# Third-level products in all pairs of the first round, index operations split over four steps, conv tiles and unit matrix in ring slots

## The chip, the cores and the metric

The kernel runs on one core of one Trainium2 chip. The metric is the device time of one execution in microseconds (us), as the median of several runs. PE is TensorE, DVE is VectorE, ACT is ScalarE, POOL is GpSimd and SP the engine whose queue issues most transfers. All data are float32.

## The reference

`x` has 32 samples of 128 channels by 2048. Two layers follow each other; cut to what matters:

```python
# layer 0
att  = softmax(mlp(cond))                               # 32 x 8
aggw = einsum('bk,koi->boi', att, weight)               # one 128 x 128 matrix per sample
y    = einsum('boi,bih->boh', aggw, x) + (att @ bias_k)[:, :, None]
x    = x + y @ W.T + bias + sum_e coeffs*scales * (y @ A_e.T) @ Bf_e.T
# layer 1
z = grouped_conv1d(x, 9 taps, 4 groups) + ctx + bias
t = z[:, perm].reshape(rows, 16 heads, 128)
t = down_h(gelu(up_h(t)))                               # 128 -> 512 -> 128 in each head
x = x + unpermuted(t)
```

The low-rank terms are added into the weights, so the dense part of layer 0 is one product of 4096 rows by a 2048 x 2048 matrix. It is taken before the 128 x 128 mixing of each sample.

## The kernel before

**The large product.** Weights and rows are cut in two by two blocks, and the product is made of seven block products instead of eight (the Winograd form of Strassen's scheme). These outer products are the seven *rounds*, in the order `ROUNDS = ("P1", "P2", "P6", "P7", "P5", "P3", "P4")`. A round runs over the eight groups `g` of four samples, so there are 56 *steps* `i`, with `i = 8 * round + g`. Inside a step the same scheme is used again: seven inner products P1 to P7, each of four 128x512 matmuls (`kc` 0 to 3) that are summed in one PSUM bank. In the profile a float32 matmul is two records. The scheme needs combined inputs. `x_combine` makes those of the rows (tile `s_P`, POOL, four operations of 128x512), `inner_weights` those of the weights (tiles `P_t`, POOL).

**The third level.** `PAIRS` names, for each round, the pairs of groups (0 is groups 0 and 1) that go a level further. In such a pair the inner products P2 and P4 of both groups are taken together as seven *quarter* products of four 128x256 matmuls each. `third_weights` prepares their weights once a round: eight POOL operations of 128x256 (tile `P_q`) at once, and four DVE operations of 128x512 put into `quarter_ops`, of which one is issued at each of the places `between(0)` to `between(3)` of the next step. `third_inputs` prepares the rows of a pair (tile `sq`, four operations of 128x512). A step of such a pair runs `multiply_third` in place of `multiply`: five products P1, P5, P6, P3, P7, and in the odd group the seven quarters too. In the rounds of `ENDS` (P1 and P4) the quarters stand after the five products, in the others between them. A quarter's result is added by one DVE operation. The result tiles of both groups are stored after the odd step. `multiply` takes seven products in the order P1, P2, P6, P5, P7, P3, P4.

A product that continues in a bank (P6 continues in the bank of P1, P3 in that of P5, and so on) can start only when the DVE or ACT operation that reads the bank's sum so far is done. This is how a late DVE operation holds up PE.

**What else stands in the steps.** The order of the instructions is the program's own order, written out by hand; each engine runs its queue in that order. Steps 0 to 5 begin with `w_make_two`, which makes two further blocks of the weights: 14 matmuls of 128x512 with a DVE addition after each (line 226), then a store to DRAM from POOL's queue. The callback `between(j)` puts further DVE work after the products. In the first round that is a `row_sums` of a weight block at j = 1 and j = 3 (line 243, two operations of 128x1024), and at j = 5 of the first four steps two additions to `wsum` (lines 1140 and 1141). At j = 2 it issues from SP the loads of the weight blocks of a later step. After each step the generator `small()` is advanced, twice a step from step 5 on: it holds small work (attention, bias, conv weights), and last of all the index operations on `row` and `orow` (lines 997 to 1005), 13 DVE operations of 128x16 in one piece.

**Memory.** Nearly all large tiles come from one pool of `SLOTS` buffers of 8 KB per partition (`slot`). A load into a reused buffer waits for the last reader of what was there. The unit matrix `ident` and the three conv tiles `cq`, `cs`, `cr` have memory of their own.

**The rest.** The last round overlaps the mixing (line 601) and the conv (line 693) with its steps; after it 128 heads of the second layer run `ffn_up` (line 837) and `ffn_down` (line 848), with gather and scatter by indirect transfers whose rows are in `row` and `orow`.

Of the kernel before, what the change touches and what calls it, by code (L numbers as in the profile page):

```python
# [8 lines left out]
FP = mybir.dt.float32  # L9
# [7 lines left out]
P = 128  # L17
B = 32
L = 2048
QW = 512  # L20
# [4 lines left out]
NPH = 4  # L25
# [6 lines left out]
GB = 4  # L32
NG = B // GB
GT = GB * P
SLOTS = 25

# [10 lines left out]


PAIRS = {
    "P1": (2, 3), "P2": (0, 1, 2), "P6": (0, 1, 2, 3), "P7": (0, 1, 2, 3),
    "P5": (0, 1, 2, 3), "P3": (0, 1, 2, 3), "P4": (0,),
}
ENDS = ("P1", "P4")
# [3 lines left out]
def adaln_ffn_kernel(  # L59
# [16 lines left out]
    nc = tc.nc  # L76

    dram = ctx.enter_context(tc.tile_pool(name="dram", bufs=1, space=DRAM))
    const = ctx.enter_context(tc.tile_pool(name="const", bufs=1))
    agp = ctx.enter_context(tc.tile_pool(name="agp", bufs=2))  # L80
    big = ctx.enter_context(tc.tile_pool(name="big", bufs=SLOTS))
    psum = ctx.enter_context(tc.tile_pool(name="psum", bufs=1, space=PSUM))
    banks = [psum.tile([P, QW], FP, name=f"bank{i}", tag=f"bank{i}") for i in range(8)]

    def slot(name, shape=(P, L)):
        return big.tile(list(shape), FP, name=name, tag="s")


    def bank():
        return banks.pop(0)  # L90

    def done(*ps):
        banks.extend(ps)
# [22 lines left out]
        for g in range(NG)  # L116
    }

    ident = const.tile([B, B], FP, name="ident", tag="ident")
    make_identity(nc, ident)  # L120
    mix = const.tile([P, KEXP, P], FP, name="mix", tag="mix")
    att_bc = const.tile([P, B * KEXP], FP, name="att_bc", tag="att_bc")
    aggb = const.tile([P, B], FP, name="aggb", tag="aggb")
# [6 lines left out]
    cs = const.tile([P, 4], FP, name="cs", tag="cs")  # L130
# [422 lines left out]
    late, ins, pms, xgs, x1ts, va, vb, hts, open_ = {}, {}, {}, {}, {}, {}, {}, {}, {}  # L553
# [135 lines left out]
    def conv_product(ps, k, i, v, first, last):  # L689

        for r, (out, rhs) in enumerate(zip(halves(ps), halves(v))):
            w = late["tw"][:, k - 1] if 1 <= k <= 4 else late["te"][:, k // 5]
            nc.tensor.matmul(  # L693
                out, lhsT=w[:, 2 * i + r], rhs=rhs,
                start=first and r == 0, stop=last and r == 1, skip_group_check=True,
            )

    def biased(out, ps, c, i, bias, scale):

        for r in range(2):  # L700
            for j in range(2):
                part = slice((2 * r + j) * NM, (2 * r + j + 1) * NM)
                b = 2 * c + j
                nc.scalar.activation(
                    out[:, part], ps[:, part], AF.Identity,
                    bias=bias[:, 2 * i + r, b : b + 1], scale=scale,
                )

    def conv_tile(c, i, name):
        return agp.tile([P, QW], FP, name=f"{name}_{c}{i}", tag=name, bufs=1)  # L710

    def conv_begin(c, i):
        px, py = bank(), bank()
        v = va[c, i]
        conv_product(px, 1, i, v[:, 0], True, False)
        conv_product(py, 3, i, v[:, 2], True, False)
        q, s = conv_tile(c, i, "cq"), conv_tile(c, i, "cs")
        biased(q, px, c, i, ctxb, 2.0)
        nc.scalar.mul(s, py, 2.0)
        open_[c, i] = px, py, q, s  # L720

    def conv_middle(c, i):
        px, py, q, s = open_[c, i]
        v = va[c, i]
        conv_product(px, 2, i, v[:, 1], False, False)
        conv_product(py, 4, i, v[:, 3], False, True)
        r = conv_tile(c, i, "cr")
        biased(r, py, c, i, ctxb, 2.0)
        nc.vector.tensor_tensor(q, q, px, ALU.subtract)
        nc.vector.tensor_tensor(s, s, py, ALU.subtract)  # L730

        nc.vector.tensor_tensor(v[:, 2], px, r, ALU.add)
        done(py)
        open_[c, i] = px, q, s, r
# [39 lines left out]
    def stage_second(c, n):  # L774
        if n in (6, 9):
            conv_middle(c, int(n == 9))
        if n in (5, 8):
            conv_inputs(c, int(n == 8), 1)
        if n in (0, 2):
            mix_begin(2 * c + n // 2)  # L780
# [5 lines left out]
    def third_products(c, n):  # L786
        if n in (5, 8):
            conv_begin(c, int(n == 8))
        if n in (6, 9):
            conv_end(c, int(n == 9))  # L790
        if n in (0, 2):
            mix_work(2 * c + n // 2)
# [71 lines left out]
        ws.append(t)  # L864

    def late_loads():
        late["tw"] = slot("tw_l", (P, 4, GR, P))
        nc.sync.dma_start(late["tw"].rearrange("p k r c -> p (k r c)"), tw_d)
        late["w1"] = slot("w1", (P, NPH, QW))
        nc.sync.dma_start(late["w1"].rearrange("p f n -> p (f n)"), w1_d.to_broadcast([P, L]))  # L870
        late["fb"] = slot("fb", (P, NPH, QW))
        nc.sync.dma_start(
            late["fb"].rearrange("p f n -> p (f n)"), fbias.to_broadcast([P, L])
        )


    def small():
# [3 lines left out]
        def take(rows, cols):  # L881
            used[0] += cols
            return sm[0:rows, used[0] - cols : used[0]]
# [8 lines left out]
        adiag = take(B, B * KEXP)  # L892
        ones = take(P, P)
        nc.gpsimd.memset(ones, 1.0)
        yield

        p0 = bank()
# [55 lines left out]
        for o in range(NPH):  # L953
# [44 lines left out]
        nc.vector.tensor_scalar(  # L998
            orow[:, 0], pos, 0x1FC, None, ALU.bitwise_and
        )  # L1000
        nc.vector.tensor_scalar(orow[:, 1], pos, 9, None, ALU.logical_shift_right)
        nc.vector.tensor_tensor(row, row, orow[:, 0], ALU.add)
        nc.vector.tensor_tensor(row, row, orow[:, 1], ALU.add)
        for g in range(NG):
            nc.vector.tensor_scalar(orow[:, g], pos, g * L, None, ALU.add)
        yield


    ctx.enter_context(tc.manual_schedule())
# [44 lines left out]
    unsummed, unsummed_first = [], list(first)  # L1054
    olds = {}
    chain = small()
    nxt, waiting, ts, quarter_ops = {}, {}, {}, []
    heads = [(g, h) for g in range(NG) for h in range(NH)]
# [5 lines left out]
    for i, (r, g) in enumerate(steps):  # L1064
# [45 lines left out]
        if last_round and g == 0:  # L1110
            quarters, quarter_ops = third_weights(r, rhs)
            late_loads()
# [148 lines left out]
```

## Time and profile before

| | us |
|---|---|
| median of 3 runs | 2588.83 (2587.49 to 2589.33) |
| profiled execution | 2590.78 |
| its span | 2589.0 |
| PE busy in the span | 2574.6 (99%) |
| DVE busy | 1514.5 (58%) |
| POOL busy | 1362.8 (53%) |
| ACT busy | 532.2 (21%) |
| first round, from its first product to its end | 45.50 to 297.83 |
| second round begins | 297.83 |

A row of a timeline gives the start in the span, the time until the group's last instruction ends, engine, line, operation, output and inputs by name, shape and count, and in brackets how long the engine stood idle before it and what ended that. Consecutive equal instructions are merged in one row. Starts that follow each other show the pace; the duration of one instruction overlaps the next one by a little.

### The profile page before, as it was taken

The numbers are of one execution on the slowest core, as the hardware profiler recorded it, in microseconds if no ns is written. First come the engines' busy times: TensorE is split into PE (matmuls) and PEld (weight loads), VectorE is DVE, ScalarE is ACT, GpSimd is POOL, SyncE is SP. The second block draws the span as 40 slices with busy tenths as digits, with TensorE's granted clock in tenths as the row PEclk, the third lists the DMA queues.
The fourth block names the chain that finished last, engine by engine and source line by source line (L and its number), as shares of the span: only waits on it lengthen the run. The fifth ranks groups of instructions, "written<-read, shape, count | busy, mean of one in ns | idle before, by whom it ended". The sixth has DMA issues, their size and how long they took to land. (4 is left out here: it accounts for less than half of the span.)

```text
span 2589.0 us, 21703 instructions
## 1 busy us (share of the span) xinstructions
PE 2574.6 (99%) x6998; PEld 1328.4 (51%) x6998; DVE 1514.5 (58%) x2368; ACT 532.2 (21%) x1099; POOL 1362.8 (53%) x1124
## 2 busy tenths in 40 slices
PE   9999999999999999999999999999999999999999
PEld 4445554455555555555554454455544454455543
DVE  5656565466555676654377666667666666666601
ACT  0000000000000000000011244444444444444432
POOL 7323756988977845977514234343444334434222
PEclk9999999999999999999999999999999999999999
DMA  7543467778467477573766887777767877787432
GB/s 324 210 163 129 162 235 317 289 296 336 187 246 296 189 316 297 199 317 156 254 229 228 256 303 254 241 243 232 228 225 234 258 232 222 226 257 234 161 127 89
DMA packets 186577, 608.30 MB, mean 235 GB/s; under 512 B 17632, under 2 KB 91872, under 8 KB 142304
## 3 DMA queue, kind: packets, MB, share of 16 engines
q1 hardware_dynamic: 147936, 473.48, 50.8%
q0 software_dynamic: 32704, 130.04, 15.0%
q10 hardware_dynamic: 5824, 3.40, 0.4%
q8 instruction: 56, 0.92, 0.1%
q14 instruction: 57, 0.47, 0.1%
HBM read 372.45 MB, written 200.84 MB: 221 GB/s over the span
## 5 line engine op out<-in xcount | busy, mean ns | idle before, releaser
L837 PE MATMUL bank<-t,ws 128*128 128x512 f32 x1024 | 460.3, 592 | 0.0
L848 PE MATMUL bank<-gl,ws 128*128 128x512 f32 x1024 | 460.2, 592 | 0.0
L855 POOL DMA_INDIRECT out<-t,orow x128 | 152.1, 1188 | 538.8 <-DVE t L853 478.6
L840 ACT ACTIVATE gl<-bank 128x512 f32<-128x512 f32 x512 | 305.8, 598 | 418.0 <-PE bank L837 415.4
L447 PE MATMUL bank<-P_t,s_P 128*128 128x512 f32 x704 | 314.5, 595 | 3.0 <-DVE p L440 3.0
L848 PEld LDWEIGHTS bank<-gl,ws 128*128 128x128 f32 x1024 | 194.6, 190 | 233.0 <-issue 231.5
L837 PEld LDWEIGHTS bank<-t,ws 128*128 128x128 f32 x1024 | 194.6, 190 | 226.6 <-issue 222.7
L586 POOL TENSOR_TENSOR x<-x,fb 128x512 f32<-128x512 f32 x128 | 177.1, 1412 | 227.5 <-DMA x<-in_x 159.5
L853 DVE TENSOR_TENSOR t<-bank,t 128x512 f32<-128x512 f32 x128 | 88.4, 690 | 325.0 <-PE bank L848 325.0
L440 DVE TENSOR_TENSOR u<-bank,u 128x512 f32<-128x512 f32 x204 | 134.0, 687 | 233.1 <-PE bank L447 214.1
L592 ACT ACTIVATE bank<-w,aggb 128x512 f32<-128x512 f32 x128 | 80.8, 684 | 867.3 <-DMA w<-w_d 855.0
L447 PE MATMUL bank<-wo_P,s_P 128*128 128x512 f32 x544 | 241.6, 592 | 0.0
L283 POOL TENSOR_TENSOR xt<-xt,xt 128x512 f32<-128x512 f32 x128 | 163.1, 1307 | 107.4 <-DMA xt<-in_xT 89.4
L447 PEld LDWEIGHTS bank<-P_t,s_P 128*128 128x128 f32 x704 | 134.3, 191 | 156.6 <-issue 152.7
L311 POOL TENSOR_TENSOR s_P<-xt 128x512 f32<-128x512 f32 x56 | 73.9, 1319 | 212.4 <-DMA xt<-in_xT 170.5
L565 DVE SCALAR_TENSOR_TENSOR ags<-mix,att_bc,ags 128x128 f32<-128x128 f32 x224 | 181.3, 810 | 4.7
L447 PEld LDWEIGHTS bank<-wo_P,s_P 128*128 128x128 f32 x544 | 103.4, 190 | 116.5 <-issue 113.6
L821 POOL DMA_INDIRECT t<-hx_d,row x128 | 131.2, 1025 | 57.0 <-issue 23.2
L440 DVE TENSOR_TENSOR p<-bank,p 128x512 f32<-128x512 f32 x84 | 56.6, 688 | 116.3 <-PE bank L447 111.6
L693 PE MATMUL bank<-va,tw_l 128*128 128x256 f32 x512 | 122.0, 380 | 2.2 <-DVE va L677 2.2
L447 PE MATMUL bank<-wo_P,xt 128*128 128x512 f32 x272 | 122.3, 592 | 0.0
L460 PE MATMUL bank<-P_q,sq 128*128 128x256 f32 x528 | 120.7, 379 | 0.4 <-DVE u L468 0.4
(191 smaller groups left out, 3515.8 us busy)
## 6 DMA issues: line engine op xcount, KB each, us to landing
xt<-in_xT SPq DMA_DIRECT2D x88, 1024.0 KB, 10.6
u<-u_d SPq DMA_DIRECT2D x40, 1024.0 KB, 10.2
wo_P<-wb_d SPq DMA_DIRECT2D x36, 1024.0 KB, 13.0
u<-c_d SPq DMA_DIRECT2D x64, 512.0 KB, 7.3
x<-in_x SPq DMA_DIRECT2D x32, 1024.0 KB, 9.3
xg<-x SPq DMA_DIRECT2D x256, 128.0 KB, 5.4
hx_d<-x1t SPq DMA_DIRECT2D x32, 1024.0 KB, 6.7
hx_d<-ht SPq DMA_DIRECT2D x32, 1024.0 KB, 4.8
```

The source lines that it names most:

```text
L283: nc.gpsimd.tensor_tensor(out[:, i, j], a[:, i, j], b[:, i, j], op)
L440: nc.vector.tensor_tensor(to, ps, to, ALU.add)
L447: nc.tensor.matmul(ps, lhsT=lhs[k][:, bass.ts(kc, P)], rhs=rhs[k][kc], start=first and kc == 0, stop=last and kc == 3, skip_group_check=True,)
L460: nc.tensor.matmul(out, lhsT=sq[k][:, i, bass.ts(kc, P)], rhs=quarters[i][k][kc], start=first and i == 0 and kc == 0, stop=last and i == 1 ...
L565: nc.vector.scalar_tensor_tensor(ag, mix[:, k], att, ag, ALU.mult, ALU.add)
L586: nc.gpsimd.tensor_tensor(xt[:, f], xt[:, f], late["fb"][:, f], ALU.add)
L693: nc.tensor.matmul(out, lhsT=w[:, 2 * i + r], rhs=rhs, start=first and r == 0, stop=last and r == 1, skip_group_check=True,)
L821: nc.gpsimd.indirect_dma_start(out=t.rearrange("p k t -> p (k t)"), out_offset=None, in_=hx_d[g].rearrange("l k t -> l (k t)"), in_offset= ...
L837: nc.tensor.matmul(pu, lhsT=w[:, m * P : (m + 1) * P], rhs=t[:, 0], start=True, stop=True)
L840: nc.scalar.activation(gl[m], pu, AF.Gelu)
L848: nc.tensor.matmul(pd, lhsT=w[:, (MC + m) * P : (MC + m + 1) * P], rhs=gl[m], start=(m == 0), stop=(m == MC - 1),)
L855: nc.gpsimd.indirect_dma_start(out=out, out_offset=bass.IndirectOffsetOnAxis(ap=orow[:, g, h : h + 1], axis=0), in_=t[:, 1], in_offset=None,)
```

## The change

- The first round takes the third level in all four pairs, not in pairs 2 and 3 alone. Steps 0 to 3 become `multiply_third`, and `third_weights` of this round runs at step 0 in place of step 4.
- The index operations are cut by further `yield`s into six pieces. As the generator is advanced twice after a step, they stand after four steps: 2, 5, 4 and 2 operations after steps 11, 12, 13 and 14.
- The three conv tiles become slices of one ring slot, taken in the last round; the unit matrix becomes a part of the tile `small` and is made on POOL after step 0 in place of the start. The ring has 26 slots in place of 25.

```diff
-SLOTS = 25
+SLOTS = 26
 PAIRS = {
-    "P1": (2, 3), "P2": (0, 1, 2), "P6": (0, 1, 2, 3), "P7": (0, 1, 2, 3),
+    "P1": (0, 1, 2, 3), "P2": (0, 1, 2), "P6": (0, 1, 2, 3), "P7": (0, 1, 2, 3),
     "P5": (0, 1, 2, 3), "P3": (0, 1, 2, 3), "P4": (0,),
 }
-    ident = const.tile([B, B], FP, name="ident", tag="ident")
-    make_identity(nc, ident)
...
-    def conv_tile(c, i, name):
-        return agp.tile([P, QW], FP, name=f"{name}_{c}{i}", tag=name, bufs=1)
+    def conv_tile(n):
+        return late["cv"][:, n]
...
-        q, s = conv_tile(c, i, "cq"), conv_tile(c, i, "cs")
+        q, s = conv_tile(0), conv_tile(1)
...
-        r = conv_tile(c, i, "cr")
+        r = conv_tile(2)
...
     def late_loads():
+        late["cv"] = slot("cv", (P, NPH, QW))
         late["tw"] = slot("tw_l", (P, 4, GR, P))
...
         nc.gpsimd.memset(ones, 1.0)
+        ident = take(B, B)
+        make_identity(nc, ident)
         yield
...
         nc.vector.tensor_scalar(
             orow[:, 0], pos, 0x1FC, None, ALU.bitwise_and
         )
+        yield
         nc.vector.tensor_scalar(orow[:, 1], pos, 9, None, ALU.logical_shift_right)
         nc.vector.tensor_tensor(row, row, orow[:, 0], ALU.add)
+        yield
         nc.vector.tensor_tensor(row, row, orow[:, 1], ALU.add)
         for g in range(NG):
             nc.vector.tensor_scalar(orow[:, g], pos, g * L, None, ALU.add)
-        yield
+            if g % 2 == 1:
+                yield
```

## The prediction

> **What bounds the kernel.** I read the page's engine sums first, then the waits of PE, then the timelines of PE, DVE and POOL around each place that the change touches, and the windows with the granted clock.
>
> ```profile
> PE 2574.6 (99%) x6998; PEld 1328.4 (51%) x6998; DVE 1514.5 (58%) x2368; ACT 532.2 (21%) x1099; POOL 1362.8 (53%) x1124
> PE bank L447 <- DVE p L440: 3.0, 1, 3.0
> PE bank L693 <- DVE va L677: 2.2, 4, 0.9
> ```
>
> PE is busy throughout, so the time moves only by PE work, PE pauses and PE's clock. The second and third lines (us in total, times, longest) are the two largest pauses inside the run; the one of 3.0 us is in the reach of the change. DVE around it:
>
> ```profile
> 390.88 1.29 DVE L440 TENSOR_TENSOR p<-bank,p 128x512 f32<-128x512 f32 x2 [1.83 <-PE bank L447]
> 392.08 1.22 DVE L997 TENSOR_SCALAR row<-pos 128x16 int32<-128x16 int32 x1
> 393.21 1.30 DVE L998 TENSOR_SCALAR orow<-pos 128x16 int32<-128x16 int32 x1
> ...
> 398.10 1.83 DVE L1005 TENSOR_SCALAR orow<-pos 128x16 int32<-128x16 int32 x8
> 399.85 0.68 DVE L440 TENSOR_TENSOR p<-bank,p 128x512 f32<-128x512 f32 x1
> ```
>
> and PE, with the window that shows its clock (the eighth value from the right block, after POOL, is PEclk):
>
> ```profile
> 390.68 3.60 PE L447 MATMUL bank<-w,xt 128*128 128x512 f32 x8
> 394.11 3.60 PE L447 MATMUL bank<-P_t,s_P 128*128 128x512 f32 x8
> 400.67 5.37 PE L447 MATMUL bank<-P_t,s_P 128*128 128x512 f32 x8 [2.97 <-DVE p L440]
> 405.88 7.03 PE L447 MATMUL bank<-w,s_P 128*128 128x512 f32 x16
> 400.00:405.00 5.00, 4.33 (x6) 1.84 (x7) 2.29 (x6) 0.00 (x0) 1.42 (x2) 0.66 1.02 362
> ```
>
> The index operations hold DVE from 392.08 to 399.85. P1's addition, which could run from about 394.4, comes after them; P6 continues in P1's bank, is due at 397.54 and starts at 400.67. After the pause PE is granted 0.66 of its clock, and this product takes 405.88 - 400.67 = 5.21 us where the one before it took 3.43.
>
> **Index operations.** Both losses go: 2.97 + (5.21 - 3.43) = 4.75 us. Each new place has its own deadline. Two operations after step 11 end at 394.43, when P1 itself has just ended: nothing. Five after step 12 cost by the same rows 394.43 to 398.10 and one blocked start more, 5.0 us; with the last additions of the step before (1.4 us) and P1's own (0.7) that is 7.1, and in step 13 P6 is due only after P1, P5 and four quarters, 2 x 3.43 + 4 x 1.73 = 13.8 us. If that step had no quarters between, P6 would be due at 6.87 and PE would lose 0.2. Four after step 13 face step 14, where P6 is due at 6.87: by L1005's eight in 1.83 us they cost 1.0 to 1.3, at 1.3 each 5.2, so 0 to 0.4 us late; I take 0, as L1005 is the same operation. The last two: 0.
>
> **PE work.** A step's seven products go from 81.55 to 105.58, 24.03 us, 3.433 each. The quarters of a pair:
>
> ```profile
> 238.44 1.03 PE L460 MATMUL bank<-w,xt 128*128 128x256 f32 x4
> 241.89 5.34 PE L460 MATMUL bank<-P_q,sq 128*128 128x256 f32 x24
> 250.52 0.97 PE L939 MATMUL bank<-small 128*128 128x32 f32 x8
> ```
>
> from 238.44 to 250.52, 12.08 us for 28 matmuls. A pair falls from 14 products (48.06) to 10 and the quarters (34.33 + 12.08 = 46.41): 1.65 us less, in two more pairs 3.30 us. This is the whole arithmetic gain.
>
> **What is added beside PE.** POOL gets eight `sq` operations of about 1.27 us and the eight `P_q` operations four steps earlier. It stood idle 20.47, 19.96 and 30.54 us before the `x_combine` of steps 2, 3 and 4, and those results are due at the second product of a later step; hidden with over 20 us to spare. DVE gets seven quarter additions of 0.69 for three product additions less per pair; a quarter lasts 1.73, so each is done before the next. The stores of `m_P` wait on SP's queue for the end of the pair, and the x load of step 3 behind them; it is issued near 108 and due near 148, against 10.6 us to land (median of `xt`). The unit matrix leaves a POOL queue that then waits 8 us for DVE anyway. The ring has one slot more until the last round and then 25 again; the order on each engine around the conv is unchanged: 0, with the four waits of L693 (2.2 us) as the bound either way.
>
> **The new wait.** It stands between steps 0 and 1. With five products step 0 ends at 45.50 + 5 x 3.433 = 62.66. PE goes on with `w_make_two`; four matmuls go to free banks, to 66.10, and the fifth continues in the first one's bank, so it waits for that one's addition on DVE. Ahead of it in DVE's queue now stand P3's addition, the fourth `P_q` operation, two row sums, P7's addition and lines 1140 and 1141. `multiply` ran the row sums and those two lines before its last products; five products leave no such room. What the items take depends on POOL:
>
> ```profile
> 191.46 0.73 POOL L393 TENSOR_TENSOR P_q<-w 128x256 f32<-128x256 f32 x1
> 196.08 1.70 POOL L399 TENSOR_TENSOR P_q<-w,w 128x256 f32<-128x256 f32 x1
> 192.77 1.09 DVE L1130 TENSOR_TENSOR P_q<-P_t,P_q 128x512 f32<-128x512 f32 x1
> 193.79 3.41 DVE L243 TENSOR_TENSOR wsum<-wsum,w 128x1024 f32<-128x1024 f32 x2
> 206.11 2.48 DVE L243 TENSOR_TENSOR wsum<-wsum,w 128x1024 f32<-128x1024 f32 x2
> 53.24 7.42 DVE L243 TENSOR_TENSOR wsum<-wsum,w 128x1024 f32<-128x1024 f32 x4
> ```
>
> Beside POOL's small `P_q` operations two row sums take 3.33 (193.79 to 197.12) and a POOL operation of 0.73 takes 1.70; with POOL quiet they take 2.39 (206.11 to 208.50); beside POOL's 128x512 operations the first three of the last row take 6.2, 2.07 each. P3's addition starts 0.27 after its product, 59.50, and the next operation 0.61 later, 60.11. Beside `P_q`: 1.05 + 3.33 + 0.61 + 1.05 + 1.66, and 0.69 for the awaited addition: 68.50, PE goes on 0.14 later, a pause of 2.54 us. Quiet: 0.60 + 2.39 + 0.61 + 0.78 + 1.23 + 0.69: 66.41, pause 0.45. Beside 128x512: 1.21 + 4.14 + 0.61 + 1.21 + 2.07 + 0.69: 70.04, pause 4.08. I take 2.54: POOL ended `x_combine` of step 1 at 58.3, its eight `P_q` operations follow and took 8.8 us from 191.46, so they lie just beside this stretch. Between steps 2 and 3 the same queue without `P_q`, with POOL quiet, ends within 0.1 us of need.
>
> **Does the clock fall again?** By the rows, pauses up to 0.9 us left it alone and one of 2.97 cost 1.78 more; 2.54 lies between, unseen. I take none, and keep 1.78 for the range. The Trainium skill, TensorE: Matmul & The Clock Gate, section "What's actually happening", puts the fall after an idle window of about 3.4 us that runs free of the kernel. This trace fell at 2.97, below that figure; by the page neither pause would cost clock, which by itself would make the sum -3.73 instead of -5.51.
>
> **Sum.** -4.75 - 3.30 + 2.54 = -5.51 us. The profiled execution, 2590.78 (span 2589.0 and 1.78 around it), becomes 2585.3; the median of the runs is 1.95 lower, so 2583.3. 0.2% is 5.2 us, about what a measurement of this kernel can tell from no change: the forecast stands just outside.
>
> **Rivals.**
> - *Free DVE.* POOL gets through earlier, the pause is 0.45: -7.60, 2581.2. For it: DVE idles before 59.5, and POOL can catch up there. Against: POOL has 8.8 us of `P_q` left at 58.3.
> - *Long pause or the clock.* 2.54 with the clock loss gives -3.73, 2585.1; 4.08 with it gives -2.19, 2586.6. For it: `P_q` on DVE and POOL already contend from 46.4 on, which makes `x_combine` end later and puts 128x512 operations beside the row sums.
> - *The index wait only moves.* The five-operation piece stops PE as the thirteen did: -3.30 + 2.54 = -0.76, 2588.1. Against: the 13.8 us above.
> - *Slower: a weight block comes late.* The second block of step 2 now reuses a buffer that is free only after the row sums behind P3 of step 1. They end at 62.66 + 2.54 + 12.02 (`w_make_two`, 69.53 to 81.55) + 4 x 3.43 + 0.27 + 0.61 + 2.39 = 94.2. Step 2 begins 12.02 + 17.17 + 12.08 after 65.20, at 106.47, and needs this block added before its sixth matmul, so landed by 110.2: 16.0 us. Loads of `in_WT` land in 11.0 (median); the slowest first load, of `a_sb`, took 24.9. Such a one would stop PE for 8.9 and cost 1.78 of clock: +5.2, 2594.0. It decides from 16 us on, and turns the sign near 21.
>
> **Numbers.** Forecast 0.45, free 0.28, long or clock 0.17, moved 0.04, slower 0.06. The forecast's own spread is about 1.5 us, two thirds of it beyond 5.2. Faster: 0.30 + 0.28 = 0.58; slower 0.06; the rest, 0.36, within. The range runs from 2580.7 (the free case with some of the L693 waits gone) to 2587.2 (the long pause with clock, and 0.6 for the waits priced at nothing); outside are the moved and the slower case and the tails.
>
> **What would show it.** Right: no index wait near 395, clock 1.00 there, steps 1 and 3 ending in 12.1 us of quarters, a PE pause at L223 near 66 released by DVE's addition to `w`, with L1141 ending just before. Wrong: no pause there (free), a pause over 3 us with a window of lower clock (long), PE waiting for a transfer near 110 (slower), or a pause near 415 or 440 behind `orow` (moved).

## The result and the profile after

The changed kernel takes 2594.2 us (median of 14 runs, 2590.76 to 2596.7) against 2588.3 (14 runs, 2586.43 to 2589.58): 1.0021 times as long, 95% interval 1.0014 to 1.0028. It is slower, where 2583.3 was forecast. The profiled execution is 2594.36 us, its span 2592.6; that of before was 2590.78, some 2.5 above the median of its 14 runs, so the two traces differ by 3.6 us and the medians by 5.9.

The engines' sums on the page after:

```profile
PE 2573.9 (99%) x7046; PEld 1339.0 (52%) x7046; DVE 1525.8 (59%) x2378; ACT 533.0 (21%) x1099; POOL 1376.2 (53%) x1132
```

PE did a little less work, and the time still grew. The waits of PE (us in total, times, longest) say where:

```profile
PE bank L221 <- DVE w L224: 4.9, 3, 2.8
PE bank L458 <- DVE u L466: 3.3, 1, 3.3
PE bank L691 <- DVE va L675: 1.3, 3, 0.6
```

Most line numbers are two lower than before. The index wait on `p` is gone. The first two rows were short before:

```profile
PE bank L223 <- DVE w L226: 0.5, 2, 0.3
PE bank L460 <- DVE u L468: 0.4, 1, 0.4
```

Now the first has 4.9 us in three places and the second 3.3 in one. PE's timeline at four places:

```profile
394.30 3.60 PE L445 MATMUL bank<-w,xt 128*128 128x512 f32 x8
397.73 4.46 PE L445 MATMUL bank<-P_t,s_P 128*128 128x512 f32 x10
...
63.00 3.60 PE L221 MATMUL bank<-bf_sb,a_sb 128*128 128x512 f32 x8
68.37 5.42 PE L221 MATMUL bank<-tb,sa 128*128 128x512 f32 x12 [1.78 <-DVE w L224]
...
208.01 3.70 PE L221 MATMUL bank<-bf_sb,a_sb 128*128 128x512 f32 x8
214.50 5.83 PE L221 MATMUL bank<-tb,sa 128*128 128x512 f32 x9 [2.80 <-DVE w L224]
...
884.19 3.60 PE L445 MATMUL bank<-P_t,s_P 128*128 128x512 f32 x8
891.12 5.18 PE L458 MATMUL bank<-P_q,sq 128*128 128x256 f32 x16 [3.33 <-DVE u L466]
```

The first two rows follow each other at PE's pace: no pause at the index operations. The third and fourth hold the pause that the forecast expected near 66. The last four hold two pauses that it did not name, one in `w_make_two` of step 5 and one in the fifth round, P5, which the diff does not touch. The windows (after POOL stands PEclk) add what those two cost in clock:

```profile
400.00:405.00 5.00, 5.00 (x13) 2.16 (x12) 2.58 (x5) 0.00 (x0) 2.75 (x3) 1.00 1.00 357
215.00:220.00 5.00, 5.00 (x9) 2.11 (x8) 3.38 (x7) 0.00 (x0) 0.00 (x0) 0.67 0.00 0
890.00:895.00 5.00, 3.88 (x11) 3.25 (x12) 4.96 (x9) 0.00 (x0) 4.84 (x5) 0.66 0.01 2
```

In each of the last two windows a third of 5 us is lost, 1.7 us. So the two new places cost 2.8 + 1.7 and 3.3 + 1.7 = 9.5 us, less the 0.3 and 0.4 us at most that PE waited there before. Set against the forecast's -5.51 that gives about +3.3, and the traces show +3.6.

**Why DVE is late at 214.** The changed kernel's DVE and POOL around it, then the same operations of the kernel before (lines 932 and 311 there are 933 and 309 here):

```profile
208.89 4.96 DVE L933 SCALAR_TENSOR_TENSOR aggb<-att_bc,small,aggb 128x32 f32<-128x32 f32 x7
213.77 3.20 DVE L224 TENSOR_TENSOR w<-bank,w 128x512 f32<-128x512 f32 x5
...
207.54 1.26 POOL L309 TENSOR_TENSOR s_P<-xt 128x512 f32<-128x512 f32 x1 [7.00 <-PE bank L445]
211.33 1.26 POOL L312 TENSOR_TENSOR s_P<-xt,s_P 128x512 f32<-128x512 f32 x1
```

```profile
209.83 2.09 DVE L932 SCALAR_TENSOR_TENSOR aggb<-att_bc,small,aggb 128x32 f32<-128x32 f32 x7
211.85 4.30 DVE L226 TENSOR_TENSOR w<-bank,w 128x512 f32<-128x512 f32 x7
...
219.80 1.27 POOL L311 TENSOR_TENSOR s_P<-xt 128x512 f32<-128x512 f32 x1 [13.47 <-PE bank L223]
```

Seven tiny operations on `aggb` take 4.96 us in place of 2.09, while POOL runs `x_combine` of step 6. One by one, the first three take 1.30, 1.19 and 1.18 us, each ending within 0.1 us of the end of a POOL operation, and the other four 0.27, after the last of POOL's. The third and the fourth of the changed kernel:

```profile
211.45 1.18 DVE L933 SCALAR_TENSOR_TENSOR aggb<-att_bc,small,aggb 128x32 f32<-128x32 f32 x1
212.67 0.27 DVE L933 SCALAR_TENSOR_TENSOR aggb<-att_bc,small,aggb 128x32 f32<-128x32 f32 x1
```

In the kernel before POOL did `x_combine` 12 us later: it stood idle 13.47 us until a product of `w_make_two` had released a buffer. With 26 buffers it still waits there, but for an earlier product and 7.00 us.

**Why DVE is late at 890.** After, and before:

```profile
882.63 1.75 DVE L419 TENSOR_TENSOR sq<-xt,xt 128x512 f32<-128x512 f32 x1
884.31 1.75 DVE L420 TENSOR_TENSOR sq<-xt,sq 128x512 f32<-128x512 f32 x1
887.18 1.31 DVE L561 TENSOR_SCALAR ags<-mix,att_bc 128x128 f32<-128x128 f32 x1
889.70 2.47 DVE L466 TENSOR_TENSOR u<-bank,u 128x512 f32<-128x512 f32 x4
...
882.24 1.60 POOL L309 TENSOR_TENSOR s_P<-xt 128x512 f32<-128x512 f32 x1
```

```profile
883.12 1.21 DVE L421 TENSOR_TENSOR sq<-xt,xt 128x512 f32<-128x512 f32 x1
886.58 0.27 DVE L563 TENSOR_SCALAR ags<-mix,att_bc 128x128 f32<-128x128 f32 x1
888.05 2.47 DVE L468 TENSOR_TENSOR u<-bank,u 128x512 f32<-128x512 f32 x4
...
849.69 1.27 POOL L254 TENSOR_TENSOR P_t<-wo_P,P_t 128x512 f32<-128x512 f32 x1 [5.62 <-PE bank L447]
882.61 1.17 POOL L399 TENSOR_TENSOR P_q<-wo_P,wo_P 128x256 f32<-128x256 f32 x1
```

Before, POOL waited 2.23 and 5.62 us for buffers of `P_t` in `inner_weights`, and so was at its small `P_q` operations when DVE did `sq`. After, it is nine microseconds further, at 128x512 operations, and `sq` and `ags` take longer beside them.

### The profile page after: what moved, and what is told of

It is laid out like the page before. It is cut to its first block, busy times and chain, and to the rows that moved or that the text cites. A ratio compares the mean times of both kernels' runs of the same rounds, so it can differ in the third digit from the quotient of the medians.

```text
span 2592.6 us, 21824 instructions
## 1 busy us (share of the span) xinstructions
PE 2573.9 (99%) x7046; PEld 1339.0 (52%) x7046; DVE 1525.8 (59%) x2378; ACT 533.0 (21%) x1099; POOL 1376.2 (53%) x1132
## 5 line engine op out<-in xcount | busy, mean ns | idle before, releaser
L445 PE MATMUL bank<-P_t,s_P 128*128 128x512 f32 x768 | 340.7, 592 | 0.0
L445 PEld LDWEIGHTS bank<-P_t,s_P 128*128 128x128 f32 x768 | 145.9, 190 | 167.5 <-issue 163.8
L563 DVE SCALAR_TENSOR_TENSOR ags<-mix,att_bc,ags 128x128 f32<-128x128 f32 x224 | 187.5, 837 | 4.7
L458 PE MATMUL bank<-P_q,sq 128*128 128x256 f32 x576 | 132.9, 382 | 3.3 <-DVE u L466 3.3
L458 PEld LDWEIGHTS bank<-P_q,sq 128*128 128x128 f32 x576 | 110.4, 192 | 35.1 <-issue 21.1
L691 PE MATMUL bank<-va,tw_l 128*128 128x256 f32 x512 | 122.0, 380 | 1.5 <-DVE va L675 1.3
```

Of the source, the lines that this page charges most:

```text
L445: nc.tensor.matmul(ps, lhsT=lhs[k][:, bass.ts(kc, P)], rhs=rhs[k][kc], start=first and kc == 0, stop=last and kc == 3, skip_group_check=True,)
L458: nc.tensor.matmul(out, lhsT=sq[k][:, i, bass.ts(kc, P)], rhs=quarters[i][k][kc], start=first and i == 0 and kc == 0, stop=last and i == 1 ...
L563: nc.vector.scalar_tensor_tensor(ag, mix[:, k], att, ag, ALU.mult, ALU.add)
L691: nc.tensor.matmul(out, lhsT=w[:, 2 * i + r], rhs=rhs, start=first and r == 0, stop=last and r == 1, skip_group_check=True,)
```

## The experiments

**Theory A:** the 26th buffer frees POOL from waits for buffers; its operations run earlier, and land beside DVE operations that they hold up. **Theory B:** the two new pairs move POOL or overload DVE, and the number of buffers is innocent.

### One part of the change at a time

`e_index` is the kernel before with the further `yield`s alone.

> The kernel before with the index operations in six places and nothing else. Both theories: the pause of 2.97 us before the product at 400.67 and the half clock after it go, 4.75 us in all, so about 2583.5 us, ratio 0.9982. If the wait only moves to one of the new places: 2587 to 2588.

Measured: 2585.03 us against 2588.64, ratio 0.9985 (0.9976 to 0.9994), 3.6 us less. At 394 us PE runs through at clock 1.00. The wait is gone and has not moved.

`e_slots` is the kernel before with the memory part of the diff alone:

```diff
-SLOTS = 25
+SLOTS = 26
...
+        late["cv"] = slot("cv", (P, NPH, QW))
...
+        ident = take(B, B)
+        make_identity(nc, ident)
```

> The kernel before with 26 buffers, the conv tiles and the unit matrix in them; pairs and index operations as before. Theory A (one buffer more lets POOL run ahead, beside short DVE chains, which then hold up PE near 211 and near 887): POOL's x_combine of step 6 starts some 10 us earlier, the aggb operations of line 933 take 1.2 us each in place of 0.27, and there is a new PE pause of about 3 us near 211 or near 887, or both: 2591 to 2597 us, beside the index pause that stays. Theory B (the two new pairs move POOL, not the number of buffers): no change, 2588.3 within 1.5, and no pause there.

Measured: 2597.07 us against 2588.64, ratio 1.0033 (1.0021 to 1.0044), at the top of what theory A gave, with the pairs as before. Its DVE, POOL and waits of PE:

```profile
209.91 4.92 DVE L933 SCALAR_TENSOR_TENSOR aggb<-att_bc,small,aggb 128x32 f32<-128x32 f32 x7
...
208.40 1.38 POOL L309 TENSOR_TENSOR s_P<-xt 128x512 f32<-128x512 f32 x1 [1.75 <-PE bank L445]
```

```profile
PE bank L458 <- DVE u L466: 3.3, 1, 3.3
PE bank L221 <- DVE w L224: 3.2, 2, 2.9
PE bank L445 <- DVE p L438: 2.9, 1, 2.9
```

Both new pauses stand beside the old index pause. The memory part alone makes them; theory B falls.

`t_pairs25` is the kernel before with the new `PAIRS` line alone.

> The kernel before with the third level in all pairs of the first round and nothing else, still 25 buffers. Theory A: the pause near 66 of 1.9 to 2.5 us stands, those near 211 and 887 do not: -3.30 + 2 = -1.3, about 2587 us. Theory B: the pauses near 211 (3.0, and 1.7 of clock) and near 887 (2.9, and 1.7 of clock) come with the pairs: -1.3 + 9.3 = +8, about 2596 us.

Measured: 2603.03 us, ratio 1.0051 (1.0038 to 1.0065), outside what either theory gave. The two pauses are indeed absent, as A says, but a third, larger one stands in step 1 (its PE, its ACT):

```profile
97.80 2.90 PE L447 MATMUL bank<-P_t,s_P 128*128 128x512 f32 x3 [13.02 <-ACT m_P L442]
...
97.07 1.07 ACT L442 COPY m_P<-bank 128x512 f32<-128x512 f32 x2 [30.31 <-DMA wb_d<-w]
```

The result tile `m_P` of step 1 finds no buffer until a store of a weight block has landed, since a pair holds both its result tiles. With 26 buffers nobody waits there. So the extra buffer is what the two pairs need, and what brings the two pauses.

`t_after25` is the changed kernel with `SLOTS = 25`, all else kept.

> The changed kernel with 25 buffers in place of 26. Theory A: the pauses near 211 and 887 go, up to 9.3 us, so 2585 us, and with them the whole of the unforeseen loss. Theory B: both stay, 2594 us.

Measured: 2601.32 us, ratio 1.0047 (1.0033 to 1.006). The two pauses are gone, the wait for `m_P` is there with 12.9 us. In this kernel the waits of POOL are back:

```profile
236.98 1.27 POOL L309 TENSOR_TENSOR s_P<-xt 128x512 f32<-128x512 f32 x1 [17.75 <-PE bank L221]
861.96 1.27 POOL L252 TENSOR_TENSOR P_t<-wo_P,P_t 128x512 f32<-128x512 f32 x1 [5.62 <-PE bank L445]
```

It has the unit matrix and the conv tiles where the changed kernel has them, so those moves alone do not make the pauses; together with `e_slots` this leaves the count of buffers. The wait of 12.9 us also shifts all that follows it; no run has the moves with 25 buffers and without that wait. The 2585 us expected of it was wrong for the same reason as above.

### Is it POOL beside DVE?

`n_comb6` takes POOL away at the first place and leaves DVE its work:

```diff
+        if (r, g) == ("P1", 6):
+            for n, t in enumerate((a21, a11, a22, a12)):
+                nc.scalar.copy(s[:, n], t)
+        else:
+            tt(s[:, 0], a21, a22, ALU.add)
...
```

> The changed kernel with the four operations of x_combine for step 6 as copies on ACT in place of additions on POOL (the additions themselves are left out). DVE has the same work at the same place; only POOL is quiet from 207 to 213. Theory A (a POOL operation with SBUF inputs holds up DVE operations with two SBUF inputs): the aggb chain takes 2.3 us in place of 5.2 and the pause near 211 goes, with its clock: 2589.5 to 2591, as f_aggb. If the chain is slow by itself, or by its place: 5.2 us, pause and 2594 stay.

Measured: 2590.89 us against 2588.63, ratio 1.0004 (0.9995 to 1.0013), 3.6 us better than the changed kernel by the ratios to before. Its DVE (lines below the edit are four higher):

```profile
209.05 2.11 DVE L937 SCALAR_TENSOR_TENSOR aggb<-att_bc,small,aggb 128x32 f32<-128x32 f32 x7
211.07 4.31 DVE L224 TENSOR_TENSOR w<-bank,w 128x512 f32<-128x512 f32 x7
```

The same seven operations at the same place take 2.11 us, and the awaited addition is in time.

`n_p5` does the like at the second place: for step 34 the `pieces` are skipped and `x_combine` is four ACT copies.

> The changed kernel with the x pieces and x_combine of step 34 (POOL from 876.8 to 888.4) as four copies on ACT; the additions are left out. DVE keeps all its work there, the four sq operations of steps 32 and 33 too. Theory A: the sq operations take about 0.7 us each in place of 1.64 to 1.75, ags 0.27 in place of 1.31, the quarter addition at 889.7 is in time, and the pause of 3.3 us and its 1.7 of clock go: 2589 to 2591. If DVE's sq operations are too much at this place whatever POOL does, the pause stays above 2 us: 2592 to 2594.

Measured: 2589.02 us against 2588.41, ratio 1.0000 (0.9991 to 1.0009), 5.3 us better. Its DVE (five lines higher):

```profile
881.36 0.68 DVE L424 TENSOR_TENSOR sq<-xt,xt 128x512 f32<-128x512 f32 x1
881.96 0.68 DVE L425 TENSOR_TENSOR sq<-xt,sq 128x512 f32<-128x512 f32 x1
883.76 0.28 DVE L566 TENSOR_SCALAR ags<-mix,att_bc 128x128 f32<-128x128 f32 x1
884.34 2.48 DVE L471 TENSOR_TENSOR u<-bank,u 128x512 f32<-128x512 f32 x4
```

`sq` falls from 1.75 to 0.68, `ags` from 1.31 to 0.28, and the pause is gone. At both places it is POOL beside DVE, shown and not only argued.

### Keeping the work and removing the pauses

`f_aggb` takes the eight `aggb` operations to the end of the next piece of `small()`:

```diff
-        nc.vector.tensor_scalar(aggb, ab[:, :, 0], bk[:, 0:1], None, ALU.mult)
...
         nc.vector.tensor_scalar(ctx34, ctxb, 0.75, None, ALU.mult)
+        nc.vector.tensor_scalar(aggb, ab[:, :, 0], bk[:, 0:1], None, ALU.mult)
...
```

> The changed kernel with the eight aggb operations two pieces of small() later, where DVE has time before anyone waits for it. Theory A (POOL's x_combine of step 6 beside the aggb chain holds up DVE, and so the product at 214): the pause near 211 goes, 3.0 us and up to 1.7 of clock, so about 2589.5 to 2591. If the addition is late for another reason (DVE has too much work in step 4 whatever POOL does), the pause stays and the time with it, 2594.

Measured: 2589.17 us against 2587.87, ratio 1.0005 (0.9996 to 1.0014): the pause near 211 is gone, 4.6 us less than the changed kernel by the differences to before.

`f_p5` gives POOL the `sq` operations of round P5's first pair:

```diff
-            sq = third_inputs(i, nc.gpsimd if r in ENDS else nc.vector)
+            sq = third_inputs(i, nc.gpsimd if r in ENDS or r == "P5" else nc.vector)
```

> The changed kernel with the four sq operations of round P5's pair 0 on POOL in place of DVE (steps 32 and 33). Theory A (POOL, 8 to 10 us early, stretches the DVE operations ahead of the quarter addition at 890): the pause near 887 of 3.3 us and its 1.7 of clock go, so 2589 to 2591. If POOL is then late itself with sq, PE waits for sq and nothing is gained: 2594 or more.

Measured: 2588.0 us, ratio 1.0000 (0.9991 to 1.0009): 5.8 less, the pause near 887 gone, no wait for `sq`.

`f_sums` issues the first steps' sums earlier:

```diff
-            if ri == 0 and j in (1, 3) and unsummed:
+            if ri == 0 and j in (1, 2 if g < 4 else 3) and unsummed:
...
-            if ri == 0 and j == 5 and unsummed_first:
+            if ri == 0 and j == 2 and unsummed_first:
```

> The changed kernel with the row sums and the additions to wsum of the first four steps one product earlier (at j = 1 and 2 in place of 1, 3 and 5), so that they do not stand behind the last product of a step that has five. The pause near 66 goes, 1.9 to 2.5 us: 2592 to 2592.5. If it is the P_q operations beside POOL that make the awaited addition late, most of it stays: 2594.

Measured: 2591.59 us, ratio 1.0015 (1.0006 to 1.0024): 2.2 less, the pause near 66 gone. The interval overlaps that of the changed kernel, so the trace shows this and not the time alone. POOL's `P_q` operations still run there, so the place of the sums in DVE's queue decides, and the expectation's other reading falls.

`f_all` has all three.

> The changed kernel with the three edits of f_aggb, f_p5 and f_sums. If the three pauses are independent and are the whole of the loss against the forecast: 2594.2 - 3.0 - 1.7 - 3.3 - 1.7 - 2 = about 2582.5 us, under both kernels (before 2588.5). If removing one moves POOL or DVE so that another place stalls: 2586 to 2590.

Measured: 2581.86 us against 2587.87, ratio 0.9974 (0.9965 to 0.9984), and 11.9 below the changed kernel where the three alone sum to 12.6. It beats both kernels. Its longest waits of PE, and its windows at the three places:

```profile
PE bank L155 <- DVE warm L152: 1.5, 1, 1.5
PE bank L691 <- DVE va L675: 1.4, 2, 0.7
PE bank L178 <- DMA bf_sb<-in_BfT: 1.4, 1, 1.4
```

```profile
65.00:70.00 5.00, 5.00 (x13) 2.13 (x12) 4.86 (x9) 0.59 (x1) 4.92 (x7) 1.00 0.01 2
210.00:215.00 5.00, 5.00 (x13) 2.19 (x12) 4.00 (x7) 0.00 (x0) 0.55 (x1) 1.00 0.00 0
885.00:890.00 5.00, 5.00 (x18) 3.15 (x17) 3.59 (x6) 0.00 (x0) 5.00 (x5) 1.00 0.00 0
```

PE is busy for all of each, at full clock.

`f_all_p23` is `f_all` with `"P1": (2, 3)`.

> The kernel f_all with the third level in pairs 2 and 3 of the first round alone, as before the change. It shows what the two new pairs are worth where nothing else is late: by the matmul count 2 x 1.65 = 3.3 us more, so 2585.2 against 2581.9 of f_all. If the pairs bring waits of their own even then, less: 2582 to 2584.

Measured: 2584.12 us against 2588.63, ratio 0.9982 (0.9973 to 0.9991). Between the medians lie 2.3 us, between the differences to before 1.5, and the intervals overlap. The traces show where the gain lies: from the first matmul of `w_make_two` of step 0 to that of step 4 are 145.00 us (33.03 to 178.03) here and 141.61 (34.33 to 175.94) in `f_all`, 3.39 less, as the matmul count says. The two whole spans differ by 1.1 us only (2582.4 and 2581.3): the trace of `f_all` began step 0 1.30 us later, and PE waited 1.9 us at L691 against 0.7. Whether the two pairs bring this about is not shown.

## Why the prediction was wrong

- **Index operations: right.** -4.75 was forecast. Between `e_slots` and the changed kernel the lead at the same matmuls grows from 0.98 to 5.53 us across this place, 4.55; `e_index` shows 3.6, interval 1.6 to 6.2.
- **PE work: right.** -3.30 was forecast, and the stretch with the pairs became 3.39 us shorter, of which the whole time shows 1.5 to 2.3. Step 2 began at 106.45, forecast 106.47; so close is chance, as PE went on 0.27 us early after the pause and took 0.25 longer from there. DVE got ten operations more, where the forecast's count gives eight; no wait came of it.
- **The pause between steps 0 and 1: right in place and cause, a little smaller.** PE went on at 68.37, forecast 68.64 (the addition's end at 68.50 and 0.14). It waited 1.78 us by the profile, or 1.94 by the pace of its matmuls, on which the forecast's 2.54 was counted, without loss of clock.
- **The failed step** is the sentence "The ring has one slot more until the last round and then 25 again; the order on each engine around the conv is unchanged: 0, with the four waits of L693 (2.2 us) as the bound either way." The order of instructions is unchanged, but not their times. The price was some 9 us, at two places far from the conv. Its companion failed too: POOL's work was called "hidden with over 20 us to spare", which asks only when its results are due, not what runs beside it when it comes earlier.
- **The row was there.** POOL's wait of 13.47 us before the `x_combine` of step 6, released by PE, is a wait for a buffer. With a buffer to spare POOL can start earlier, in `e_slots` at 208.40, and so beside the eight `aggb` operations at 209.5. The prediction itself priced DVE operations of 0.60 us at 1.21 beside POOL's 128x512. By that price, 0.6 us more for each of seven, an estimate is that PE could be held up 4 us; with the loss of clock this place alone would have taken back the forecast gain.
- **The rivals.** None had this mechanism. *Slower* named 2594.0, near the result, but by a weight block that comes late near 110; PE waited for no transfer there. The nearness is chance. *Long pause or the clock* was wrong in its place: the pause near 66 stayed short and cost no clock. *Free DVE* and *the index wait moves* did not happen.
- **What stays open.** Why POOL runs 8 to 10 us earlier in P5 is traced to its waits for `P_t`; which readers hold which buffers there was not followed one by one. The changed kernel's runs spread over 6 us, and the clock goes with it: the nine with a mean granted clock of 0.998 took 2593.57 to 2596.7 us, the five with 0.999 took 2590.76 to 2593.29. This suggests that the two pauses do not cost clock in every run; which of them did is known for the one traced run alone.

## What to carry to other kernels

A buffer more is not a term of zero: list the waits for buffers that it removes, put the released engine's work at its new time, and ask what runs beside it there. An engine with idle time can still hurt by when it works; here POOL did the same additions 12 us earlier and stopped PE. Short chains on DVE that stand just ahead of an addition that PE awaits are the ones to move away first.

## What the runs showed of the hardware

- **DVE beside POOL.** Seven operations of 128x32 with two arrays in SBUF as inputs took 4.92 to 4.96 us beside POOL and 2.09 to 2.11 with POOL quiet; `sq` of 128x512 fell from 1.75 to 0.68 us. How short the operation is does not protect it: in the changed kernel three of the seven took 1.18 to 1.30 us, about as long as one POOL operation of 128x512 (1.26), and the four after POOL's last took 0.27. The Trainium skill, SBUF — State Buffer, section "Who interferes with whom", says that a DVE instruction with two SBUF inputs contends with a GpSimd instruction that reads SBUF, and calls the port pair that they share an exclusive lock. The rows agree: `aggb` and `sq` were held, and two additions from a bank to SBUF, one SBUF input each, took 1.27 us beside POOL and 1.28 with POOL quiet (the operations just ahead of `ags` in the changed kernel and in `n_p5`). The first operation on `ags`, with one array and one number per partition as inputs, was held too, 1.31 us against 0.28; why is not shown.
- **Pauses and clock.** The wait of 1.8 us near 66 left the clock at full in the changed kernel. The same wait of 2.8 us in step 5 was followed by half clock in the changed kernel (0.67 from 215 to 220) and in `n_p5` (0.66), and not in `f_p5` and `f_sums` (1.00), where the same addition was late by the same time. The record of the clock in the traces shows what differs. In the changed kernel half clock begins at 214.89, at 890.73 and, after the last product, at 2590.57: 198 and 498 times 3.413 us apart, so the clock changes on a fixed grid of windows. The wait of 2.8 us lies in one window in the changed kernel and in `n_p5`; in `f_p5` an edge splits it into 1.97 and 0.83 us, in `f_sums` into 1.59 and 1.22. In the thirteen traces every wait inside the run with 2.0 us or more in one window was followed by half clock, and none with 1.97 or less (2.0 in `e_slots`, 1.97 in `f_p5`; the next on either side are 2.3 and 1.77). After a wait of about 3 us half clock lasts one window, which costs 1.7 us.
- **A long wait.** In `t_pairs25` a wait of 13.0 us showed 0.50 from 92 to 97, 0.55 from 97 to 102 and 1.00 after: half clock for some 3.7 us after PE had gone on at 97.8, hardly more than the 3.4 after a wait of 2.8. In these two cases the loss of clock is about the same, whatever the length of the wait. The Trainium skill, TensorE: Matmul & The Clock Gate, section "What's actually happening", has a window of 3.4 us that runs free of the kernel, which agrees with the grid. It puts the fall after at least one idle window of that length; here the clock fell after waits of 2.8 us, so in this case the measurement decides.
